# Last graph layer: the edge weights of a node group kept in the PSUM bank of its own sum

## The chip, the cores and the metric

The kernel runs on one core of a Trainium2 chip. The time is the device time of one execution in microseconds (us). Before the change the median of 13 runs is 5820.31 us (5806.52 to 5838.92).

The core has five engines that run their own instruction queues in order and wait for each other through semaphores: PE (matrix products, with PEld for the loading of its stationary operand), DVE (elementwise work and reductions), ACT (activations and copies), POOL (here mostly the issue of indirect DMAs, which gather rows of a table) and SP (plain DMAs). SBUF is the on-chip memory, PSUM the accumulator memory of PE: eight banks of 512 float32 values in each of 128 partitions.

## What is computed

The reference is a stack of four graph layers, each followed by a feed-forward layer, on 3125 nodes of 256 features. The change touches only the last graph layer, an attention over incoming edges with 8 heads of 32 features:

```python
h = (x @ W.T).reshape(n, H, D)                      # H = 8, D = 32
alpha = einsum(h_src, a_src) + einsum(h_dst, a_dst)
enc = relu(edge_attr @ edge_W.T + edge_b).reshape(-1, H, D)
alpha = alpha + sum(enc * h_dst, axis=-1)
alpha = where(alpha >= 0, alpha, 0.2 * alpha)
amax = segment_max(alpha, dst)
ex = exp(alpha - amax[dst])
denom = segment_sum(ex, dst)
attn = ex / maximum(denom[dst], 1e-10)
out = segment_sum(h_src * attn[..., None], dst).reshape(n, H * D) + bias
```

The result is added to x, normalised per node, and goes to the last feed-forward layer, which sends each node to two of eight experts.

## The kernel before

**Tiling.** The nodes are sorted by their number of incoming edges and cut into NT = 25 groups of 128, one node to a partition. Group g has KS[g] edge slots per node, from 41 in group 0 and 25 in group 1 down to 10 in group 24. A slot of a group is a 128 x 264 tile: 256 features of the edge's source and 8 partial scores. Slots go in chunks of C4 = 4, so there are 123 chunks: 104 of four slots, 6 of three, 6 of two and 7 of one.

**The loop.** `pipeline` (L1091) goes through all chunks of all groups in order, one chunk a turn. In a turn it first issues the gathers of up to two chunks: POOL fetches their slots from the table TA (L1082, 428 gathers of 128 rows in all), some six turns ahead and into 14 buffers `gt`. Then come the steps of the chunk and the score of the chunk before. The order in each engine's queue is the order in which the program is written out; no scheduler changes it.

- `enc_ahead` (L3101): ACT copies edge attributes (L3016), PE transposes them for eight slots into the first 128 columns of the PSUM tile `small` (L3026), ACT copies them out (L3035, L3039), and PE multiplies them with the edge weights (L3052) into `e_ps`, a PSUM tile with four buffers of one bank, two slots each.
- `score` (L3056): DVE takes relu and multiplies by the target's features, two slots an instruction (L3062), sums each head's 32 features into L, 8 scores a slot (L3065), and adds the gathered partial scores (L3066).
- When a group's last chunk has been scored, `tail` (L3075) is put beside the loop and advances by one step a turn. It adds the target's score and the leaky slope (L3077, L275) and calls `weigh`.

**`weigh`** (L1719) does the softmax and the weighted sum of one group. DVE adds a penalty for empty slots (L1725), takes the maximum (L1727, L1729) and subtracts it (L1730). ACT takes the exponential (L1734), for 8 heads in place, in the SBUF tile L. A turn later DVE sums the weights into `den` (L1739), and then in each turn multiplies one chunk of gathered features by its weights into an SBUF tile `wv` with four buffers (L1769). PE sums a chunk's four slots by four products with the identity into the PSUM tile `acc` (L1752; two records each in the trace, as the product is float32). In a turn the weighting of chunk k is written ahead of the matmuls of chunk k-1 (`summed`, L1748). Groups of more than six chunks, which are groups 0 and 1, take two chunks a turn. At the end `tail` divides by `den` (L3081 to L3084) and adds bias and sum to X (L3086, L3087). After each fifth group the normalisation of five groups runs beside the loop, with the product for the gate (L112) into further columns of `small`.

The helper `weigh` serves three layers. In the first layer (4 heads, then 1) it is given `exps`, and for 4 heads the exponentials are written to a PSUM tile `expo` of a bank of its own (L1734, read at L1739 and L1769). The last layer gives it none.

**PSUM in the last layer.** `tps2` one bank, `small` one, `e_ps` four, `acc` two buffers of 256 columns. A tile that is written by one engine and read by another is guarded by semaphores; `acc` has two buffers, so group g+2 reuses group g's.

Of the kernel before, what the change touches and what calls it, by code (L numbers as in the profile page):

```python
# [11 lines left out]
F32 = mybir.dt.float32  # L12
# [8 lines left out]
P = 128  # L21
D = 256
KD = D // P
N = 3125
NT = (N + P - 1) // P
# [16 lines left out]
def parts(tc, a, k, X, XNT):  # L42
# [17 lines left out]
    def spread(ap, shape):  # L60
        return ap[:, :, None].to_broadcast(shape)
# [318 lines left out]

    def first_of(pool, s, best, iota_e, E, name):

        oh = pool.tile([P, s.shape[1], E], F32, name=name)
        at = pool.tile([P, s.shape[1]], F32, name=name + "_at")
        nc.vector.tensor_tensor(oh, s, spread(best, [P, s.shape[1], E]), ALU.not_equal)
        nc.vector.scalar_tensor_tensor(oh, oh, 1000.0, iota_e, op0=ALU.mult, op1=ALU.add)
        nc.vector.tensor_reduce(at, oh, AX.X, ALU.min)
        nc.vector.tensor_tensor(oh, iota_e, spread(at, [P, s.shape[1], E]), ALU.is_equal)
        return oh

    def places(pool, E):
        iota_e = pool.tile([P, NT, E], F32, name="iota_e")
        nc.gpsimd.iota(iota_e, pattern=[[0, NT], [1, E]], base=0, channel_multiplier=0,
                       allow_small_or_imprecise_dtypes=True)
        return iota_e
# [629 lines left out]
E = 53125  # L1025
# [470 lines left out]
def quick(ctx: ExitStack, tc: tile.TileContext, a: dict, out: bass.AP, k):  # L1496
# [92 lines left out]
    E3, F3, R3 = 8, 1024, 2 * P  # L1589
# [123 lines left out]
    def chunks(g):  # L1713
        return [(c, min(C4, KS[g] - c)) for c in range(0, KS[g], C4)]
# [4 lines left out]
    def weigh(pool, psum, g, L, H, tiles, own=0, exps=None, bias=None):  # L1719


        K = KS[g]
        Z = K - own
        by_head = L.rearrange("p k h -> p h k")
        nc.vector.tensor_add(L[:, :Z, :], L[:, :Z, :], pen[:, OFF[g] : OFF[g] + Z, None].to_broadcast([P, Z, H]))  # L1725
        mx = pool.tile([P, H], F32, name="mx")
        nc.vector.tensor_reduce(mx, by_head, AX.X, ALU.max)  # L1727
        if not own:
            nc.vector.tensor_scalar_max(mx, mx, -0.5 * BIG)  # L1729
        nc.vector.tensor_sub(L, L, mx[:, None, :].to_broadcast([P, K, H]))  # L1730
        E = L
        if H == 4:
            E = exps(g, K * H).rearrange("p (k h) -> p k h", h=H)
        nc.scalar.activation(E, L, AF.Exp)  # L1734
        yield 0
        if own:
            nc.vector.tensor_scalar(E[:, Z, :], E[:, Z, :], 2.0, None, op0=ALU.mult)
        den = pool.tile([P, H], F32, name="den")
        nc.vector.tensor_reduce(den, E.rearrange("p k h -> p h k"), AX.X, ALU.add)  # L1739
        if H == 4:  # L1740
            nc.vector.reciprocal(den, den)
            nc.vector.tensor_mul(E, E, den[:, None, :].to_broadcast([P, K, H]))
        acc = psum.tile([P, D], F32, name="acc", bufs=2)
        if bias is not None:
            nc.tensor.matmul(acc, ident, bias, start=True, stop=False)
        held = []

        def summed():  # L1748
            for c, n, wv, t in held:
                for s in range(n):  # L1750
                    w, v = (wv[:, s, :P], t[:, s, :D]) if H == 1 else (ident, wv[:, s, :])
                    nc.tensor.matmul(acc, w, v, start=(c + s == 0 and bias is None), stop=(c + s == K - 1))  # L1752
            held.clear()


        todo = list(zip(chunks(g), tiles))
        per = 2 if len(todo) > 6 else 1
        for i in range(0, len(todo), per):
            made = []
            for (c, n), t in todo[i : i + per]:  # L1760
                wv = pool.tile([P, C4, D], F32, name="wv", bufs=4)
                if H == 1:
                    nc.vector.tensor_mul(wv[:, :n, :P], exps[:, None, :].to_broadcast([P, n, P]),  # L1763
                                         E[:, c : c + n, :].to_broadcast([P, n, P]))
                else:
                    x = t[:, :n, :D].rearrange("p s (h c) -> p s h c", h=H)
                    if H == 4:
                        x = t[:, :n, : D + H].rearrange("p s (h c) -> p s h c", h=H)[:, :, :, : D // H]
                    nc.vector.tensor_mul(wv[:, :n, :].rearrange("p s (h c) -> p s h c", h=H), x,  # L1769
                                         E[:, c : c + n, :, None].to_broadcast([P, n, H, D // H]))  # L1770
                made.append((c, n, wv, t))
            free = len(held) if H == 1 else len(made)
            summed()
            held.extend(made)
            yield free
        free = len(held) if H == 1 else 0
        summed()
        weighed[g] = acc, den
        yield free
# [3 lines left out]
    def gat(H, table, own_rows, att, fixed, expo, gp, mp, sp, psum, opened, finish, beside=None, ranked=0,  # L1783
# [55 lines left out]
        def tail(g):  # L1839
            if H == 1:  # L1840
                yield 0
            yield from weigh(sp, psum, g, st[g].L, H, list(st[g].tiles.values()), 1, exps, bias)
            st.pop(g)
            yield from finish(g, *weighed.pop(g))
# [384 lines left out]
    with tc.tile_pool(name="rt", bufs=1) as rt_pool:  # L2229
# [6 lines left out]
        H, C, INNER = 8, 64, 512  # L2236
# [183 lines left out]
        H, C = 4, 4  # L2420
# [6 lines left out]
        with tc.tile_pool(name="rg", bufs=12) as gp, tc.tile_pool(name="rs", bufs=2) as sp, \  # L2427
# [13 lines left out]
            def tail(g, acc):  # L2441
                nc.vector.scalar_tensor_tensor(X[:, g, :], acc, 0.5 ** 0.5, X[:, g, :], op0=ALU.mult, op1=ALU.add)
                nc.vector.tensor_add(X[:, g, :], X[:, g, :], hb)
                if g % BATCH < BATCH - 1:
                    return
                yield 0
                gs = range(g - BATCH + 1, g + 1)
                yield from norm_pieces(sp, psum, gs)
                tbs = []
                for g_ in gs:  # L2450
                    ps = psum.tile([P, HC], F32, name="hg_ps", bufs=2)
                    f.node_matmul(ps, g_, wg, slice(0, HC))
                    tb = sp.tile([P, GW], F32, name="tb", bufs=2 * BATCH)
                    tv = tb[:, : H * (C + 1)].rearrange("p (h c) -> p h c", h=H)
                    nc.vector.memset(tb, 1.0)
                    nc.vector.tensor_copy(tb.bitcast(I32)[:, H * (C + 3) : H * (C + 3) + 1], place[:, g_ : g_ + 1])
                    nc.scalar.copy(tv[:, :, :C], ps.rearrange("p (h c) -> p h c", h=H))
                    m = sp.tile([P, 2, HC], F32, name="m2")
                    nc.vector.tensor_mul(m, ps[:, None, :].to_broadcast([P, 2, HC]), at_r)
                    nc.vector.tensor_reduce(tb[:, H * (C + 1) : H * (C + 3)],  # L2460
                                            m.rearrange("p s (h c) -> p (s h) c", h=H), AX.X, ALU.add)
                    tbs.append(tb)
                    yield 0
                yield 0
                yield 0
                for g_, tb in zip(gs, tbs):
                    scatter(tc, "gm", gm, pid(g_), tb)
                    yield 0
# [453 lines left out]
    H, C = 8, 32  # L2922
# [17 lines left out]
    with tc.tile_pool(name="ag", bufs=abufs) as gp, tc.tile_pool(name="am", bufs=2) as mp, \  # L2940
# [39 lines left out]
        HS = lgs[:, :, :H]  # L2980

        tps2 = psum.tile([P, 2, KD, P], F32, name="tps2")
        small = psum.tile([P, P + NT * E3], F32, name="small")
        halves = itertools.cycle(range(2))
        turns = SimpleNamespace(tile=lambda *_, **__: tps2[:, next(halves), :, :])
        for gs in batches():
# [16 lines left out]
        tiles, Ls, atts, es, logits = {}, {}, {}, {}, {}  # L3003
# [71 lines left out]
        def tail(g):  # L3075
            L = Ls.pop(g)
            nc.vector.tensor_add(L, L, HD[:, g : g + 1, D:].to_broadcast([P, KS[g], H]))  # L3077
            f.leaky(L, L)
            yield from weigh(sp, psum, g, L, H, tiles.pop(g))
            acc, den = weighed.pop(g)  # L3080
            nc.vector.tensor_scalar_max(den, den, 1e-10)  # L3081
            nc.vector.reciprocal(den, den)
            h = sp.tile([P, D], F32, name="h")
            nc.vector.tensor_mul(h.rearrange("p (h c) -> p h c", h=H), acc.rearrange("p (h c) -> p h c", h=H),  # L3084
                                 den[:, :, None].to_broadcast([P, H, C]))
            nc.vector.tensor_add(X[:, g, :], X[:, g, :], bias)  # L3086
            nc.vector.tensor_add(X[:, g, :], X[:, g, :], h)  # L3087
            if g % BATCH == BATCH - 1:
                yield 0
                yield from norm_pieces(sp, turns, range(g - BATCH + 1, g + 1), XN, (gate, gated))  # L3090
                b = slice(g - BATCH + 1, g + 1)
                nc.sync.dma_start(top_xn[b.start * P : b.stop * P, :].rearrange("(t p) d -> p t d", p=P), XN[:, b, :])
# [195 lines left out]
```

## Time and profile before

| what | value |
|---|---|
| median of 13 runs | 5820.31 us |
| profiled execution: time, span | 5837.86 us, 5835.9 us |
| last layer: first gather, last accumulating matmul | 4603 us, 5325 us |
| busy over the span: PE, DVE, ACT, POOL | 58%, 53%, 21%, 49% |
| gathers of the last layer (L1082) | 428, 432.9 us, mean 1011 ns |
| weighting of the last layer (L1769) | 123, 138.8 us, mean 1135 ns |
| accumulation of the last layer (L1752) | 906 records, 289.7 us, mean 474 ns |
| scores (L3062) and their sums (L3065) | 233, 147.2 us; 123, 139.7 us |
| exponentials (L1734) in the last layer | 25, 8.1 us |
| sums of the weights (L1739) in the last layer | 25, 10.1 us |

How to read it: the span is one execution as the hardware profiler saw it, from its first to its last instruction. Busy times count the engines' own instructions, not waits. Groups are told by line, engine and operation, with a tile's name for its output and inputs; a line can be that of a helper, so L1769 stands in the page both for the first layer and for the last, and only a stretch of time tells them apart. "Idle before" is the time that the engine stood still just ahead of a group's instructions, with what ended it. The clock is the share of full speed that TensorE was granted.

### The profile page before, as it was taken

The numbers are of one execution on the slowest core, as the hardware profiler recorded it, in microseconds if no ns is written. First come the engines' busy times: TensorE is split into PE (matmuls) and PEld (weight loads), VectorE is DVE, ScalarE is ACT, GpSimd is POOL, SyncE is SP. The second block draws the span as 40 slices with busy tenths as digits, with TensorE's granted clock in tenths as the row PEclk, the third lists the DMA queues.
The fourth block names the chain that finished last, engine by engine and source line by source line (L and its number), as shares of the span: only waits on it lengthen the run. The fifth ranks groups of instructions, "written<-read, shape, count | busy, mean of one in ns | idle before, by whom it ended". The sixth has DMA issues, their size and how long they took to land.

```text
span 5835.9 us, 43920 instructions
## 1 busy us (share of the span) xinstructions
PE 3360.3 (58%) x12989; PEld 2304.6 (39%) x13034; DVE 3093.9 (53%) x6063; ACT 1219.2 (21%) x3088; POOL 2881.7 (49%) x3076
## 2 busy tenths in 40 slices
PE   2334553355487964545347556059679355556996
PEld 1223333234354532434124333035354233334885
DVE  4577877798675754651114331473441567876001
ACT  1222223455531200000013232121112101111221
POOL 4567664577765036675644535430403566661323
PEclk9676777676798976666668777579885677777998
DMA  4534342233321233332212221253324333332554
GB/s 122 158 103 108 107 114 83 79 98 110 100 31 43 113 95 93 87 87 76 29 35 77 51 60 25 67 155 103 119 79 122 98 88 87 92 90 69 190 191 161
DMA packets 320900, 553.70 MB, mean 95 GB/s; under 512 B 101962, under 2 KB 221885, under 8 KB 317311
## 3 DMA queue, kind: packets, MB, share of 16 engines
q0 software_dynamic: 124240, 295.98, 19.9%
q1 hardware_dynamic: 189973, 248.17, 12.9%
q10 hardware_dynamic: 6422, 6.48, 0.4%
q8 instruction: 112, 1.84, 0.1%
q14 instruction: 153, 1.25, 0.1%
HBM read 434.55 MB, written 118.86 MB: 95 GB/s over the span
## 4 chain that ended last, share of the span: by engine, by line
PE 25%; DVE 22%; issue 19%; another core or an unknown queue 14%; POOL 10%; DMA 3%; ACT 3%; SPq 0%; DVEq 0%; ACTq 0%; POOLq 0%
POOL gt L1082 5%; PE acc L2761 3%; PE hx_ps L112 3%; DVE m L1820 3%; DVE m L1828 3%; DVE wv L1769 3%; POOL rp_g L1082 3%; PE x_o L2626 3%; PE x_ps L2612 3%; PE acc L2764 2%; PE acc L1752 2%; PE acc L1863 2%; DVE m L3062 2%; DVE L L3065 1%
## 5 line engine op out<-in xcount | busy, mean ns | idle before, releaser
L1082 POOL DMA_INDIRECT gt<-T,recs x856 | 899.5, 1051 | 464.7 <-issue 335.8
L1752 PE MATMUL acc<-wv,ident 128*128 128x256 f32 x1812 | 562.2, 466 | 290.6 <-DVE wv L1769 217.3
L1082 POOL DMA_INDIRECT gt<-rel,relz x428 | 413.6, 966 | 436.8 <-issue 368.2
L1082 POOL DMA_INDIRECT gt<-gm,recs x428 | 405.5, 948 | 420.5 <-DVE L L275 207.1
L1752 PEld LDWEIGHTS acc<-wv,ident 128*128 128x128 f32 x1812 | 416.5, 237 | 411.9 <-DVE wv L1769 167.5
L1082 POOL DMA_INDIRECT gt<-TA,recs x428 | 432.9, 1011 | 277.7 <-issue 116.6
L1752 PE MATMUL acc<-gt,wv 128*128 128x256 f32 x906 | 301.0, 493 | 315.5 <-DVE wv L1763 213.5
L1863 PE MATMUL acc<-gt,ident 128*128 128x256 f32 x856 | 288.5, 472 | 173.3 <-issue 149.6
L2633 DVE TENSOR_TENSOR x_y<-x_o,x_b 128x512 f32<-128x512 f32 (+1 forms) x52 | 34.4, 670 | 638.4 <-remote 250.1
L1752 PEld LDWEIGHTS acc<-gt,wv 128*128 128x128 f32 x906 | 215.1, 248 | 394.3 <-issue 163.0
L2761 PE MATMUL acc<-XNT,adj_g 128*128 128x512 bf16 x955 | 331.3, 392 | 49.4 <-issue 40.0
L2612 PE MATMUL x_ps<-XNT,x_w 128*128 128x512 f32 (+1 forms) x448 | 243.3, 675 | 186.5 <-ACT x_h L2614 125.6
L1823 ACT ACTIVATE m<-m 128x1024 f32<-128x1024 f32 (+3 forms) x246 | 243.5, 990 | 507.6 <-DVE m L1820 271.0
L1820 DVE TENSOR_TENSOR m<-gt,R 128x1040 f32<-128x1040 f32 (+6 forms) x246 | 281.9, 1146 | 105.0 <-DMA gt<-T,recs 70.9
L2764 PE MATMUL acc<-F,adj_g 128*128 128x256 bf16 x1000 | 279.3, 280 | 38.1 <-issue 30.1
L1863 PEld LDWEIGHTS acc<-gt,ident 128*128 128x128 f32 x856 | 196.1, 237 | 253.4 <-issue 191.8
L1828 DVE TENSOR_TENSOR m<-m,fixed 128x1040 f32<-128x1040 f32 (+6 forms) x246 | 280.4, 1140 | 23.7 <-ACT m L1823 19.1
L1082 POOL DMA_INDIRECT gt<-gcn,z_i x120 | 119.4, 995 | 315.5 <-DVE F L2736 166.7
L2626 PE MATMUL x_o<-x_w,x_h 128*128 128x256 f32 x800 | 209.9, 405 | 70.0 <-issue 70.0
L2612 PEld LDWEIGHTS x_ps<-XNT,x_w 128*128 128x128 f32 x448 | 92.0, 230 | 279.5 <-issue 143.5
L3183 PE MATMUL fh_ps<-xt,w 128*128 128x256 f32 x896 | 201.0, 383 | 0.8 <-DVE xt L3175 0.8
L3196 PE MATMUL fo_ps<-w,ht 128*128 128x256 f32 x896 | 198.0, 379 | 0.0
(653 smaller groups left out, 7037.4 us busy)
## 6 DMA issues: line engine op xcount, KB each, us to landing
w<-in_L_ffn_W_dram SPq DMA_DIRECT2D x56, 1024.0 KB
adj_g<-adj SPq DMA_DIRECT2D x40, 800.0 KB
rel<-hx SPq DMA_DIRECT2D x25, 1024.0 KB
adj<-em_a SPq DMA_DIRECT2D x20, 800.0 KB
gt<-T,recs POOLq DMA_INDIRECT x856
y<-each_d SPq DMA_DIRECT2D x25, 512.0 KB
each_d<-x_y SPq DMA_DIRECT2D x24, 512.0 KB
R<-rr SPq DMA_DIRECT2D x25, 388.5 KB
```

The lines of the kernel that those rows point to most:

```text
L1082: return nc.gpsimd.indirect_dma_start(out=out_, out_offset=None, in_=table, in_offset=index(idx))
L1752: nc.tensor.matmul(acc, w, v, start=(c + s == 0 and bias is None), stop=(c + s == K - 1))
L1820: nc.vector.tensor_add(m[:, :n, :], st[g].tiles[c][:, :n, :W], st[g].R[1][:, None, :].to_broadcast([P, n, W]))
L1823: nc.scalar.activation(v, v, AF.Abs)
L1828: nc.vector.tensor_mul(m[:, :n, :], m[:, :n, :], att_row[:, None, :].to_broadcast([P, n, W]))
L1863: nc.tensor.matmul(accs[g], ident, t[:, s, :], start=False, stop=(last and s == n - 1))
L2612: nc.tensor.matmul(ps[:, :n], ws[e][0][:, c, f_ * P : (f_ + 1) * P], XNT[:, c, c0 : c0 + n], start=(c == 0), stop=(c == KD - 1))
L2626: nc.tensor.matmul(ps[:, j, :], ht[:, f_, (i + j) * P : (i + j + 1) * P], ws[e][1][:, f_, :], start=(f_ == 0), stop=(f_ == FC - 1))
L2761: nc.tensor.matmul(acc.rearrange("p s d -> p (s d)"), A[:, b, :], F12[:, b, :, :].rearrange("p s d -> p (s d)"), start=(b == 0), stop=Fals ...
L2764: nc.tensor.matmul(acc[:, 0, :], A[:, b, :], F3_[:, b, :], start=False, stop=(b == NT - 1), skip_group_check=True)
L3183: nc.tensor.matmul(ps[:, i, :], ld[j][1][:, c, (f_ + i) * P : (f_ + i + 1) * P], xt[j][:, c, :], start=(c == 0), stop=(c == KD - 1))
L3196: nc.tensor.matmul(ps[:, i, :], h[:, f_, i * P : (i + 1) * P], w2[:, f_, :], start=(f_ == 0), stop=(f_ == FC3 - 1))
```

## The change

The tile `acc` of the last layer becomes a whole bank of 512 columns, and is taken before the exponentials instead of after. Columns 0 to 255 are the sum as before; columns 256 onward take the group's weights, 8 to a slot, which ACT now writes there instead of to L. `den` and the weightings read them from there. Group 0 has 41 x 8 = 328 weights, more than the 256 free columns. Its weights go to the last 328 columns of `small`, which grows from 328 to 512 columns; the first 184 stay free of them. The first layer's code is as before.

```diff
         nc.vector.tensor_sub(L, L, mx[:, None, :].to_broadcast([P, K, H]))
+        acc = psum.tile([P, 512], F32, name="acc", bufs=2) if H == 8 else None
         E = L
         if H == 4:
             E = exps(g, K * H).rearrange("p (k h) -> p k h", h=H)
+        if H == 8:
+            room = acc[:, D : D + K * H] if K * H <= 512 - D else exps[:, 512 - K * H :]
+            E = room.rearrange("p (k h) -> p k h", h=H)
         nc.scalar.activation(E, L, AF.Exp)
...
-        acc = psum.tile([P, D], F32, name="acc", bufs=2)
+        acc = acc[:, :D] if H == 8 else psum.tile([P, D], F32, name="acc", bufs=2)
...
-        small = psum.tile([P, P + NT * E3], F32, name="small")
+        small = psum.tile([P, 512], F32, name="small")
...
-            yield from weigh(sp, psum, g, L, H, tiles.pop(g))
+            yield from weigh(sp, psum, g, L, H, tiles.pop(g), exps=small)
```

## Prediction

> **What bounds the kernel now.** I read first the page's chain of waits, then the busy times by stretch, the waits and the groups of the last graph layer alone, and last its timeline. One line of the chain:
>
> ```profile
> PE 25%; DVE 22%; issue 19%; another core or an unknown queue 14%; POOL 10%; DMA 3%; ACT 3%; SPq 0%; DVEq 0%; ACTq 0%; POOLq 0%
> ```
>
> No engine holds the kernel as a whole, so the stage that the change touches has to be read by itself. The last layer's edge work runs from 4603 us (first gather) to 5325 us (last accumulating matmul). Two of its stretches (columns: stretch, length, busy time and count of PE, PEld, DVE, ACT, POOL, then clock, DMA share, GB/s):
>
> ```profile
> 4900.00:5100.00 200.00, 123.29 (x448) 85.73 (x447) 162.15 (x304) 22.51 (x77) 132.00 (x128) 0.77 0.33 93
> 5255.00:5326.00 71.00, 49.02 (x181) 34.96 (x179) 64.09 (x147) 10.75 (x30) 10.66 (x16) 0.76 0.10 27
> ```
>
> DVE is busy 81% and 90%, PE 62% and 69%, POOL 66% and 15%. Who waits for whom, from 4660 us on (total, times, longest):
>
> ```profile
> DVE m L3062 <- remote: 55.8, 9, 16.6
> DVE wv L1769 <- remote: 23.1, 2, 14.5
> DVE L L3066 <- DMA gt<-TA,recs: 1.2, 1, 1.2
> ...
> POOL gt L1082 <- DVE wv L1769: 107.3, 25, 12.8
> ```
>
> POOL waits 107 us for DVE to give back gather buffers; DVE waits 1.2 us for gathers. So DVE sets the pace, apart from about 90 us in which it waits for something that the profile can't name ("remote", before instructions whose inputs are ready).
>
> **What is changed, part by part.** Set side by side, the two built programs have the same instructions in the same order on all five engines. What differs is where 25 exponentials (L1734) write, where 25 sums (L1739) and 123 weightings (L1769) read, and the semaphore waits that follow from it.
>
> *The weighting itself.* Its second operand moves from SBUF to PSUM. The first layer has this very form, its weights being in a PSUM tile:
>
> ```profile
> L1769 DVE TENSOR_TENSOR wv<-gt,expo 128x1024 f32<-128x1024 f32 x104 | 125.5, 1214 | 33.1 <-remote 24.0 <-issue 6.7
> L1769 DVE TENSOR_TENSOR wv<-gt,L 128x1024 f32<-128x1024 f32 x104 | 126.2, 1219 | 36.4 <-remote 23.1 <-PE e_ps L3052 13.3
> ```
>
> 1214 against 1219 ns: 104 x 5 ns is half a microsecond, taken as nothing. [...] Sums and exponentials: the same two layers have, at 88 elements, 250 ns from PSUM and 301 ns from SBUF (L1739; four and eight outputs), and 248 and 277 ns (L1734, a write to PSUM and to SBUF). 25 x 30 ns is under 1 us, hidden in ACT's idle time; without cover it would be a gain of 0.7 us.
>
> *The gathers.* One turn of the pipeline in the timeline (start, length, engine, line, operation):
>
> ```profile
> 4943.10 1.22 DVE L1769 TENSOR_TENSOR wv<-gt,L 128x1024 f32<-128x1024 f32 x1
> 4943.27 1.87 POOL L1082 DMA_INDIRECT gt<-TA,recs  x1 [0.30 <-issue]
> 4944.24 1.02 DVE L3062 SCALAR_TENSOR_TENSOR m<-e_ps,XN 128x512 f32<-128x512 f32 x2
> ...
> 4944.37 1.99 PE L1752 MATMUL acc<-wv,ident 128*128 128x256 f32 x8 [1.39 <-DVE wv L1769]
> 4945.29 0.95 DVE L3065 TENSOR_REDUCE L<-m 128x24 f32<-128x768 f32 x1
> 4945.45 0.95 POOL L1082 DMA_INDIRECT gt<-TA,recs  x1 [0.30 <-issue]
> ...
> 4946.43 1.22 DVE L1769 TENSOR_TENSOR wv<-gt,L 128x1024 f32<-128x1024 f32 x1
> 4946.70 1.77 POOL L1082 DMA_INDIRECT gt<-TA,recs  x1 [0.30 <-issue]
> ...
> 4947.70 1.99 PE L1752 MATMUL acc<-wv,ident 128*128 128x256 f32 x8 [0.79 <-DVE wv L1769]
> ```
>
> A gather is 0.95 us; one that starts while a weighting runs is 1.77 or 1.87. Counted over the stage, 66 of 428 start during a weighting, 44 of them are slow, and their excess over 0.95 sums to 25.4 us. In the first layer, whose weighting reads PSUM, 91 gathers start during one and none is slow. So the change takes 25 us off POOL. But POOL is the engine that waits: DVE gets at most its 1.2 us, and a little where the chain crosses to POOL for a few gathers (4982 to 4987, 5066 to 5083, 5202 to 5219). Bounds 0 and 8 us, taken 2, near the waits' row.
>
> *The new waits.* The built program treats the bank as one thing. The weights now share it with the sum, so (a) the four matmuls of chunk k-1 (L1752), which waited for weighting k-1, wait for weighting k, the last reader before them in the order; and (b) weighting k+1 on DVE waits until those matmuls are done. Before, four wv buffers kept (b) off. Behind the waiting weighting stand DVE's next scores (L3062, L3065), and for them POOL's buffers; behind the waiting matmuls stand the attribute transposes (L3026) and encodings (L3052).
>
> [...] The sum uses only the waits as built.
>
> Price of (b): from weighting k to k+1 DVE needs 1.22 (the weighting) + 0.06 (end to matmul, 4940.50 to 4940.56) + 1.99 (the batch) + up to 0.10 (back) = 3.37 us. What DVE has there now, from the start times: 3.81 where a full chunk of four is scored between, 3.33 with three, 2.72 with two, 2.19 with one (4943.10 to 4946.43; 4782.94 to 4785.66; 4846.44 to 4848.63). So full turns hide it, and the short ones lose 0.04, 0.65 and 1.18. Of the 57 such intervals in groups 2 to 22, most contain other work or gaps; three at 2.72 and four near 2.2 are bare: 2.0 + 4.7 = 6.7 us. That is with warm matmuls. After an idle spell the same eight records take 3.6 to 3.8 us (4878.73: 3.78), and then even a full turn loses 1.3. Putting the length of the batch recorded behind each weighting in place of 1.99 gives 19.6 us in 18 intervals. Bounds 6.7 and 19.6; I take 14, since the weighting's wait keeps PE no idler than now, but PE is cold after each DVE gap.
>
> *Groups 0 and 1* go two chunks a step, so eight matmuls, 3.6 to 6.6 us, stand between pairs. From the starts 4704.47, 4708.30, 4713.29 and 4716.63 the last weighting of group 0 would slip 6.4 us, and group 1 some 3; group 0's weights also share the bank of the transposes. DVE has gaps of 14.5 and 8.6 us before and 13.3 us after. Bounds 0 and 10, taken 5.
>
> *The end* has no other work to hide it:
>
> ```profile
> 5318.31 1.22 DVE L1769 TENSOR_TENSOR wv<-gt,L 128x1024 f32<-128x1024 f32 x1
> ...
> 5319.67 1.97 PE L1752 MATMUL acc<-wv,ident 128*128 128x256 f32 x8 [0.96 <-DVE den L3081]
> ...
> 5321.08 1.82 DVE L1769 TENSOR_TENSOR wv<-gt,L 128x1024 f32<-128x1024 f32 x2
> 5322.36 2.86 PE L1752 MATMUL acc<-wv,ident 128*128 128x256 f32 x12 [0.72 <-DVE wv L1769]
> ```
>
> The last two groups run their last two weightings back to back. Now the batch stands between: in group 24 the batch of 5319.67 starts only at 5322.3, the third weighting at 5324.4, and the last 12 records end at 5327.9, not 5325.2: +2.7. Group 23 loses 2.3 the same way: 5 in all. The routing behind it waits for the last group, so all of it counts.
>
> **Sum:** 14 + 5 + 5 = 24. Less 4 (bounds 0 and 8) that DVE's unnamed gaps give back, where a late instruction finds its block already there; less 2 for gathers: +18. On the profiled execution's 5837.9 us (span 5835.9) that is 5856; it stands 17.6 above the median 5820.3, to which the same +18 gives **5838 us**, 0.3% slower.
>
> **Rivals.**
> *Swallowed.* DVE's unnamed gaps (55.8 + 23.1 + 11.7 + 2.9 = 93.5 us) come at fixed moments, and every stall before one disappears. Only the end stays: 5825. For: the gaps are seven times the stalls. Against: they fall at about ten places, and the stalls at others.
> *PE becomes the pace.* 27 batches of eight records are now over 3.0 us long. If each costs the full 1.3, not only the bare ones: 35 + 6.7 + 5 + 5 - 4 - 2 = +46, so 5866. For: DVE now feels each hiccup of PE. Against: batches in long intervals have room.
> *Faster.* The gathers set the pace after all and the whole 25.4 us comes back, with only the end's 5 lost: 5800. It decides from the point where DVE would otherwise wait at L3066 for landings. For: POOL runs without a break over long stretches. Against: 1.2 us of such waits.
>
> **Chances.** Forecast 0.52, swallowed 0.22, PE 0.13, faster 0.13. About 0.2% (11.6 us) is what a measurement here tells from no change: slower is above 5832. A little of the forecast's case (0.04) lies below that: slower 0.61, same 0.26, faster 0.13. The forecast's own range is 5820.3 + 6.7 + 0 + 5 - 8 - 8 = 5816 to 5820.3 + 19.6 + 10 + 5 = 5855; it already takes in swallowed, and to leave out no more than 2 in 10 I stretch it to 5814 and 5861.
>
> **What would show it.** In the profile after: weightings of 1.21 to 1.22 us; no slow gather starting in one, POOL's mean for gt<-TA near 0.95; a new wait DVE wv <- PE acc of 15 to 30 us in total; PE waiting for weighting k, not k-1; POOL's wait for wv still about 100 us or more; the stage longer by about 18 us, the last matmul some 5 us further from the last den. The forecast is wrong if DVE's wait for acc is under 8 us, if POOL's wait for wv shrinks along with the stage, or if the weighting's duration moves.

## The result and the profile after

Changed: 5887.51 us (median of 14 runs, 5866.58 to 5902.29). Before, beside it: 5826.84 us (62 runs, 5806.52 to 5852.16). The ratio is 1.0103 with a 95% interval of 1.0091 to 1.0115: slower by some 60 us, where +18 was forecast and 5861 was the upper end of the range. The profiled execution's span went from 5835.9 to 5892.9 us, +57.0.

Where these 57 us lie, by the starts of the same weightings in both traces: the first weighting of the last layer comes 5.2 us later (work that is the same in both), from there to the last accumulating matmul 658.2 us have become 711.1 (+52.9), and what follows is 1.1 us shorter. Within the stage: groups 0 and 1 +16.4, groups 2 to 22 +26.8, groups 23 and 24 +9.7.

The busy times of the stage, before and after (columns: stretch, length, busy time and count of PE, PEld, DVE, ACT, POOL, then clock, DMA share, GB/s):

```profile
4660.00:5325.00 665.00, 381.62 (x1342) 260.21 (x1342) 510.65 (x962) 70.70 (x236) 391.66 (x390) 0.75 0.30 83
```

```profile
4665.00:5383.00 718.00, 381.33 (x1342) 259.23 (x1342) 510.57 (x962) 72.27 (x237) 365.84 (x391) 0.74 0.28 76
```

DVE works the same 510.6 us in both, so all 53 us are idle time of DVE. POOL works 25.8 us less, and nobody gains by it. The groups of the stage and the waits after (second fence: total, times, longest):

```profile
L1773 DVE TENSOR_TENSOR wv<-gt,acc 128x1024 f32<-128x1024 f32 x94 | 114.0, 1216 | 46.3 <-PE acc L1756 24.6 <-remote 15.7 <-issue 6.0
L1773 DVE TENSOR_TENSOR wv<-gt,small 128x1024 f32<-128x1024 f32 x10 | 11.8, 1215 | 23.1 <-remote 23.1
```

```profile
DVE wv L1773 <- remote: 58.4, 8, 14.6
DVE m L3066 <- remote: 56.3, 18, 10.8
DVE wv L1773 <- PE acc L1756: 32.3, 23, 3.8
...
PE acc L1756 <- DVE wv L1773: 208.3, 57, 15.7
...
POOL gt L1082 <- DVE wv L1773: 156.2, 41, 13.7
```

The same wait of the sums before:

```profile
PE acc L1752 <- DVE wv L1769: 59.2, 32, 7.7
```

The weighting itself is as long as before (1216 and 1215 against 1219 ns). The wait that was forecast is there: DVE's weightings wait 32.3 us for the sums, the sums 208.3 us for weightings (59.2 before). What was not forecast is that the unnamed waits grew too: DVE's were 55.8 + 23.1 + 11.7 + 2.9 = 93.5 us and are 58.4 + 56.3 + 12.1 + 3.5 + 3.3 = 133.6. Before, the weighting waited twice for something unnamed, now eight times. The waits named as PE's encodings fell from 28.9 to 0.7 us. So most of the waiting of the scores for PE is still there, and a new one of the weightings has come on top.

Two steady turns after (start, length, engine, line, operation):

```profile
5030.23 1.22 DVE L1773 TENSOR_TENSOR wv<-gt,acc 128x1024 f32<-128x1024 f32 x1 [1.19 <-PE acc L1756]
5031.50 1.99 PE L1756 MATMUL acc<-wv,ident 128*128 128x256 f32 x8 [0.56 <-DVE wv L1773]
5033.53 1.22 DVE L1773 TENSOR_TENSOR wv<-gt,acc 128x1024 f32<-128x1024 f32 x1 [0.50 <-issue]
...
5034.81 1.99 PE L1756 MATMUL acc<-wv,ident 128*128 128x256 f32 x8 [0.88 <-issue]
```

Weighting, sums and weighting follow each other hand to hand, 3.30 us apart. And the end:

```profile
5374.67 1.21 DVE L1773 TENSOR_TENSOR wv<-gt,acc 128x1024 f32<-128x1024 f32 x1
...
5376.03 3.60 PE L1756 MATMUL acc<-wv,ident 128*128 128x256 f32 x8 [2.53 <-DVE wv L1773]
5379.66 0.69 DVE L1773 TENSOR_TENSOR wv<-gt,acc 128x512 f32<-128x512 f32 x1 [3.78 <-PE acc L1756]
...
5380.41 2.86 PE L1756 MATMUL acc<-wv,ident 128*128 128x256 f32 x12 [0.78 <-DVE wv L1773]
```

The last weighting waits 3.78 us for a batch that takes 3.60, not the 1.97 of before. PE had just stood idle for 2.53 us. The clock (the figure before the last two) of the first steady batch and of this one:

```profile
5031.50:5033.49 1.99, 1.99 (x9) 1.63 (x10) 1.41 (x3) 0.00 (x0) 1.47 (x2) 1.00 0.33 87
5376.03:5379.63 3.60, 3.60 (x8) 2.49 (x8) 0.00 (x0) 0.00 (x0) 0.00 (x0) 0.54 0.00 0
```

A batch of eight records is called cold here when it runs at about half the clock and takes over 3 us. In this trace such batches follow idle time: 27 of the 29 batches of four slots that come behind an idle PE of 2.4 us or more are cold, and 4 of the 60 that come behind less than 1 us. Before it was 5 of 9 and 22 of 72, so the idle time just ahead of a batch is not all that decides.

### The profile page after: what moved, and what is told of

Read it like the earlier page. It is cut to its first block, busy times and chain, and to the rows that moved or that the text cites. A ratio compares the mean times of both kernels' runs of the same rounds, so it can differ in the third digit from the quotient of the medians.

```text
span 5892.9 us, 43923 instructions
## 1 busy us (share of the span) xinstructions
PE 3369.8 (57%) x12989; PEld 2309.4 (39%) x13034; DVE 3094.3 (53%) x6063; ACT 1219.0 (21%) x3088; POOL 2856.1 (48%) x3076
## 4 chain that ended last, share of the span: by engine, by line
PE 26%; DVE 24%; issue 19%; another core or an unknown queue 13%; POOL 9%; DMA 3%; ACT 3%; DVEq 0%; POOLq 0%; SPq 0%; ACTq 0%
POOL gt L1082 5%; PE acc L2765 3%; DVE m L1824 3%; PE acc L1756 3%; DVE wv L1773 3%; DVE m L1832 3%; PE hx_ps L112 3%; PE x_ps L2616 3%; POOL rp_g L1082 3%; PE x_o L2630 3%; PE acc L2768 2%; DVE m L3066 2%; DVE L L3069 1%; DVE L L1837 1%
## 5 line engine op out<-in xcount | busy, mean ns | idle before, releaser
L1756 PE MATMUL acc<-wv,ident 128*128 128x256 f32 x1812 | 579.1, 478 | 446.0 <-DVE wv L1773 358.4
L1082 POOL DMA_INDIRECT gt<-TA,recs x428 | 406.9, 951 | 344.8 <-DVE wv L1773 156.2
```

What stands on the lines that cost most here:

```text
L1082: return nc.gpsimd.indirect_dma_start(out=out_, out_offset=None, in_=table, in_offset=index(idx))
```

## The experiments

The rounds of runs fell on five chips, and these are of two kinds. On three the kernel before takes 5799 to 5829 us, as it does in the first comparison; on two it takes 5127 and 5129. So only ratios to the kernel before on the same chip are compared.

**First theory: the loop of two waits** (sums of chunk k-1 held until weighting k has read, weighting k+1 held until they are done). Four kernels, on a chip where the kernel before takes 5127.15 us. Sums emitted first:

```diff
         for i in range(0, len(todo), per):
+            if H == 8:
+                summed()
             made = []
```

> The changed kernel, with the matmuls of chunk k-1 emitted ahead of the weighting of chunk k instead of behind it. Every engine has the same instructions in the same order; the bank is still shared, and weighting k still waits for the matmuls of chunk k-1, but these no longer wait for weighting k. Theory L (the loop: matmuls held until the next weighting has read, and the weighting after it until they are done, costs the 60 us): most of it goes, 5827 + 5 at the last two groups + 0 to 10 = 5832 to 5842, ratio 1.001 to 1.003. Rival W (any wait of a weighting for matmuls in the bank costs it): 5870 or more, ratio 1.008 and up. Rival O (the operand in PSUM, through faster gathers or slower neighbours, costs it, and no wait): 5887, ratio 1.010.

Measured: 5188.02 us, ratio 1.0120 [1.0105, 1.0136]. The first theory (1.001 to 1.003) falls: without the one half of the loop the loss in per cent is as large as in the first comparison (the changed kernel itself was not run on this chip). The program as built shows why: weighting k now waits for the sums of chunk k-1, and these for weighting k-1. As this program and the changed one are built, sums and weightings in the shared bank wait for each other, so either of the two orders leaves one handover in each turn: here PE's sums wait 77.8 us in 55 waits for weightings, and DVE's weightings 80.1 us in 37 for sums. In DVE's waits of this stage nothing is unnamed on this chip:

```profile
DVE wv L1775 <- PE acc L1756: 80.1, 37, 5.9
```

The timeline of this kernel shows one of them:

```profile
4261.86 0.16 DVE L3079 TENSOR_TENSOR lg<-small,bg 128x8 f32<-128x8 f32 x1
4262.07 1.02 PE L112 MATMUL small<-wg,XNT 128*128 128x8 f32 x4 [3.69 <-DVE lg L3079]
...
4262.95 0.67 PE L1573 MATMUL tps<-ident,XN 128*128 128x128 f32 x2
...
4263.41 3.62 PE L1756 MATMUL acc<-wv,ident 128*128 128x256 f32 x8
...
4267.07 1.22 DVE L1775 TENSOR_TENSOR wv<-gt,acc 128x1024 f32<-128x1024 f32 x1 [5.05 <-PE acc L1756]
```

The sums stand in PE's queue behind the gate and a transpose; the gate waits 3.69 us for DVE; then the batch takes 3.62 us, at a granted clock of 0.50; and DVE waits 5.05 us for it. The direct path of weighting and sums is only a part of this round. Worked out from the starts in this trace: had each of the 37 batches begun 0.06 us behind its weighting, up to 57 of the 80.1 us would be gone; had each taken 1.99 us, up to 29 (20 of them are cold); the two overlap.

Weights in a bank of their own, made room for by putting both accumulators in one bank (the companion has this alone):

```diff
+        if H == 8 and g:
+            E = wts[:, g % 2, : K * H].rearrange("p (k h) -> p k h", h=H)
...
-        acc = psum.tile([P, D], F32, name="acc", bufs=2)
+        acc = exps[:, g % 2, :] if H == 8 else psum.tile([P, D], F32, name="acc", bufs=2)
...
+        acc2 = psum.tile([P, 2, D], F32, name="acc2")
+        wts = psum.tile([P, 2, D], F32, name="wts")
```

> Weights of groups 1 to 24 in a PSUM bank of their own (two halves by group), room for it made by putting both accumulators in one bank; group 0's weights in SBUF. Weightings read PSUM as in the changed kernel, but share no bank with matmuls. Theory L and rival W: no loss by the operand, so the time of the kernel with both accumulators in one bank (its companion here) within 6 us, ratio to before 0.998 to 1.003. Rival O: about 40 to 60 us above that companion, ratio 1.008 or more. If the gathers set the pace after all: 10 to 25 us below the companion.

> The kernel before with both accumulators in one PSUM bank and nothing else: the price of making room. A group's first matmul now waits until the group before has been read (once per group, 24 times). All theories: 0 to 10 us, ratio 1.000 to 1.002.

Measured: own bank 5111.69 us, 0.9966 [0.9952, 0.9979]; companion 5126.67 us, 0.9997 [0.9988, 1.0006]. The room is free, and the operand in PSUM is no loss here but a gain of 15 us, as was expected for the case that the gathers set the pace (10 to 25 below the companion). Rival O falls. In the companion DVE waits 15.8 us in 20 waits for landings of gathers, with the own bank 2.7 in 4.

Two buffers for weighted rows, weights in SBUF:

```diff
-                wv = pool.tile([P, C4, D], F32, name="wv", bufs=4)
+                wv = pool.tile([P, C4, D], F32, name="wv", bufs=2 if H == 8 else 4)
```

> The kernel before, weights in SBUF, with two buffers for weighted rows instead of four: weighting k+1 waits for the matmuls of chunk k-1, as in the changed kernel, but these do not wait for weighting k. Theory L: 0 to 10 us, ratio 1.000 to 1.002. Rival W: this wait alone gives most of the loss, 40 us or more, ratio 1.007 and up. Rival O: 0 to 10 us.

Measured: 5134.74 us, 1.0015 [1.0006, 1.0024]. Weighting k+1 waits for the same sums as in the changed kernel, but these may start one turn earlier. Rival W (1.007 and up) falls: not any wait for the sums is dear. With a turn of slack the wait costs 8 us; without it, in the kernel with the sums first, the loss is 61 (there with the operand in PSUM).

**Second theory: one handover a turn, and it is the wait, not the bank.** Four kernels on another chip (before 5798.79 us). The changed kernel again; with group 0's weights in SBUF; with only groups 2 to 22 sharing:

```diff
-        if H == 8:
+        if H == 8 and 2 <= g < NT - 2:
```

and the waits alone, in SBUF, with one buffer for weighted rows per parity of the group:

```diff
+            if H == 8:
+                summed()
...
+                wv = pool.tile([P, C4, D], F32, name=f"wv{g % 2}", bufs=1) if H == 8 and per == 1 else \
+                    pool.tile([P, C4, D], F32, name="wv", bufs=2 if H == 8 else 4)
```

> The changed kernel as it is, beside the others of this round. Theory R (one handover a turn: with the bank shared, the matmuls and the weightings of a group can only take turns, and the matmuls stand behind encodings and transposes that wait for ScalarE, so the whole round trip between DVE and PE falls into every turn): the same as with the sums emitted first, since either order has one handover a turn, so ratio 1.010 to 1.014. If the first theory (the loop of two waits) still has something to it: clearly above the 1.012 of that kernel, 1.016 or more.

> The changed kernel with group 0's weights left in SBUF, so that the bank of the transposes holds no weights. Theory R: group 0 has two chunks a turn and is one of 25, so 0 to 10 us below the changed kernel. Rival T (the waits on the transposes' bank, which hold PE for 25 us in the profile of the changed kernel, are the main price): 30 us or more below it.

> The changed kernel with the weights of groups 0, 1, 23 and 24 left in SBUF, so that only the steady middle (groups 2 to 22) shares its banks. Theory R: 5 to 20 us below the changed kernel, ratio to before still 1.007 or more. Rival E (the price lies at the two ends of the stage, where nothing covers a wait): ratio 1.003 or less.

> The kernel before, its weights in SBUF, with the sums emitted ahead of the weighting and a single buffer for weighted rows per group of each parity (two where a turn takes two chunks): weighting k waits for the matmuls of chunk k-1 in every turn, exactly the waits of the shared bank with the sums first, but DVE and PE never use a PSUM bank together. Theory R: the waits are the whole price, so ratio 1.009 to 1.015. Rival H (the chip itself holds up one engine while the other uses the bank): clearly less, 1.004 or below.

Measured: changed 5853.18 us, 1.0087 [1.0068, 1.0106]; group 0 out of it 5840.96, 1.0075 [1.0058, 1.0093]; steady middle only 5830.32, 1.0057 [1.0042, 1.0072]; waits alone 5844.50, 1.0075 [1.0058, 1.0092]. By the medians the +54 divides into 12 for group 0 (a little over what was expected, and its interval overlaps), 11 for groups 1, 23 and 24, and 32 for the middle. The ratios of the changed kernel, of the middle and of the waits alone lie 0.0013 to 0.0015 below their expected bounds, inside their intervals; the middle alone is 23 us below the changed kernel, where 5 to 20 were expected. The rival that the ends hold the price falls, though 23 of the 54 us do lie in groups 0, 1, 23 and 24. That a hold-up in the bank itself is the price falls too: with the weights in SBUF, the waits of the order with the sums first lose 46 us. That order is not the changed kernel's; but in the changed kernel's trace the weightings (1216 ns) and the sums at full clock (1.99 us) are no longer than before, either.

**Is it PE's queue?** The sums moved to the head of PE's turn, in front of transposes, encodings and gate (before 5829.48 us on this chip):

```diff
         def enc_ahead(g, c, n, last):
+            for s in early:
+                s()
```

> The changed kernel with the matmuls of chunk k-1 moved to the head of PE's turn, in front of the transposes, the encodings and the gate instead of behind them; bank, weights and handovers stay. Theory Q (the price comes from what PE has queued between a weighting and its sums: with the sums first in the queue the round trip lies beside the scoring on DVE): ratio to before 0.998 to 1.003. Rival D (weighting and batch alone, with cold batches of 3.4 to 3.8 us, are too long for a turn, wherever the sums stand): 1.006 or more, within 0.004 of the 1.009 to 1.010 of the changed kernel.

> The kernel before with the same move of the sums to the head of PE's turn, weights in SBUF: what the move does by itself. Theory Q and rival D: little, since four buffers for weighted rows keep the sums off DVE's path, ratio 0.997 to 1.003. If the encodings, which now come later in the turn, are DVE's real supply: above 1.004.

> The kernel with the weights in a PSUM bank of their own, once more, beside the others of this round and perhaps on another chip. If its gain came from gathers that no longer run slow: 0.995 to 0.999 again. If that gain needs a chip on which DVE waits for nothing but gathers: 0.998 to 1.003 here.

> Weights in a bank of their own and the sums at the head of PE's turn. No wait between weighting and sums is left for the move to shorten: within 0.003 of the kernel with the own bank. If the move helps through PE's order alone, as much below it as the kernel before with the move is below the kernel before.

Measured: changed with the move 5871.65 us, 1.0082 [1.0061, 1.0104]; before with it 5845.10, 1.0031 [1.0015, 1.0048]; own bank 5845.29, 1.0032 [1.0018, 1.0046]; own bank with the move 5868.08, 1.0082 [1.0062, 1.0102]. Two expectations failed: theory Q's of 0.998 to 1.003 for the changed kernel with the move, and that the move makes no odds to the own bank (it adds 0.005). The kernel before with the move and the own bank lie just above their bounds of 1.003. So the move costs 16 to 23 us by itself, and the own bank is slower than before on this chip. The changed kernel's 1.0082 is thus what the direct-path rival forecast, but not for its reason: the kernel without any sharing has the same 1.0082. The move also puts the sums ahead of the next weighting, so it has to be compared with the kernels that have the sums first. With the sums at the head of PE's queue, sharing the bank adds 3.6 us to the own bank, nothing that can be told apart; with the sums first but behind the rest of the queue it added 76 on the quicker chip (5111.69 to 5188.02), and the waits alone add 48 on a chip like this one (next part). That speaks for the queue in the kernels with the sums first. The comparison goes across chips, it doesn't reach the changed kernel's own order, and the move loses by itself what it saves in waits.

**How the loss divides.** Room, operand, sharing, and the waits alone, on one more chip (before 5822.44 us); the edits are those above:

> Both accumulators in one bank, weights in SBUF, on the same chip as the next three. Theory R: nothing, 0.998 to 1.002, so that what the own bank costs is the operand's. Rival A (on a chip on which PE crawls, the wait of a group's first matmul for the group before costs): 1.002 to 1.005, and the own bank's price is this one.

> Weights in a bank of their own. On a chip where DVE has waits without a name: 1.001 to 1.005 as on the last one, on a chip without: 0.995 to 0.998. Theory R: in either case clearly below the changed kernel, by 0.5% or more.

> The changed kernel. Theory R: what it has over the own bank is the handover, 0.5 to 0.8% on a chip with unnamed waits, 1.2 to 1.6% on one without (there the sums emitted first were 1.5% over the own bank).

> The waits alone, weights in SBUF. Theory R: 1.006 to 1.009 on a chip with unnamed waits, 1.010 to 1.015 on one without. Rival H (a hold-up in the shared bank itself): 1.004 or less.

| kernel | us | ratio to before | 95% interval | adds |
|---|---|---|---|---|
| accumulators in one bank | 5823.97 | 1.0007 | 0.9992 to 1.0023 | room: +2 |
| weights in a bank of their own | 5845.07 | 1.0046 | 1.0024 to 1.0067 | operand in PSUM: +21 |
| changed | 5897.66 | 1.0118 | 1.0092 to 1.0144 | sharing: +53 |
| waits alone, weights in SBUF | 5870.66 | 1.0081 | 1.0060 to 1.0101 | +48 on before |

The room costs nothing that can be told from noise, so rival A falls. Sharing is the larger part, and the copy of the waits in SBUF, in the order with the sums first, is worth about the same. The 53 us are 0.9% of the own bank's time, where 0.5 to 0.8% were expected, and they include group 0, whose weights the own bank leaves in SBUF (12 us in the round before). The smaller part is the operand, and its sign depends on the chip: +21 here, -15 on the chip of the first round.

**Why the operand helps or hurts.** One small memset on POOL after each chunk's gathers, with the weights in their own bank, gives POOL back the time that the faster gathers save:

```diff
+            nc.gpsimd.memset(idle, 0.0)
```

> Weights in a bank of their own, and after each chunk's gathers a small memset on POOL (123 of about 0.2 us, some 25 us in all, about what the slow gathers took before). If the earlier gathers make the difference: back to the kernel before, 0.998 to 1.002, on either kind of chip. If something else in the operand does: the same as its companion without memsets within 0.002.

> The companion, weights in a bank of their own, no memsets: 1.002 to 1.006 on a chip with unnamed waits, 0.995 to 0.998 on one without.

Measured, on the second of the two quicker chips (before 5129.14 us): padded 5120.85 us, 0.9985 [0.9976, 0.9994]; companion 5110.51 us, 0.9965 [0.9951, 0.9979]. The memsets take 223 ns each, and DVE's waits for landings go from 2.7 back to 9.7 us. So 10 of the 19 us hang on POOL's time for the gathers. The ratio lies at the lower edge of the first expectation (0.998) and at the upper edge of the second (0.002 above the companion), so it doesn't decide between them, and the other 8 us have no shown cause. Why the operand costs 21 us on the slow kind of chip stays open: this pair did not fall on one. In the traces there, DVE's waits in the stage grow from 137 us (both accumulators in one bank) to 154 (weights in their own), nearly all of it in what the profile calls "issue" (3.3 to 16.9 us): time in which it names nothing that was waited for.

## Why the prediction was wrong

- *What bounds the stage.* Right: DVE's busy time is 510.6 us before and after, and everything lost is idle time of DVE.
- *The weighting.* Right: 1215 and 1216 ns from PSUM.
- *The gathers.* What was forecast of them came: some 60 gathers start during a weighting and none is slow, the mean fell from 1011 to 951 ns, and POOL's wait for weightings grew (107.3 to 156.2 us) instead of shrinking. Before, with both operands of the weighting in SBUF, 36 of the gathers that start during one take over 1.2 us, the longest 1.99, and none of the 354 others over 1.14; after, with one operand in PSUM, the longest beside a weighting takes 0.95. What in the operand makes the difference was not shown. But the price, "bounds 0 and 8 us, taken 2" as a gain, had the wrong sign: with no sharing, the operand costs 21 us on one such chip (5823.97 to 5845.07), and operand and room 16 on another. The range had no loss in it. (Counted by the starts in the trace, 74 gathers rather than 66 began during a weighting before; their excess over 0.95 us is 25.5 us, as forecast.)
- *The new waits, the step that failed.* The forecast said: "from weighting k to k+1 DVE needs 1.22 (the weighting) + 0.06 (end to matmul) + 1.99 (the batch) + up to 0.10 (back) = 3.37 us", and took 14 us between 6.7 and 19.6 for the middle, "since the weighting's wait keeps PE no idler than now". In groups 2 to 22 weightings wait 22.3 us for sums by name (24.0 and 23.7 in the two other profiled executions of the changed kernel), more than the upper bound. The 3.37 is right where the batch runs at full clock (3.30 at 5030.23 to 5033.53). But the wait does keep PE idler, just ahead of its sums: these now wait 208.3 us for weightings (59.2 before). Cold batches are only a few more, but now DVE waits for them to their end. Of the 23 named waits in the whole stage 17, with 22.0 of the 32.3 us, are for batches at a clock of 0.50 to 0.55; the four for batches at full clock cost about 1 us each. Worked out from the starts: had each batch taken 1.99 us, up to 20.4 of the 32.3 us would be gone; had each begun 0.06 us behind its weighting, 3.7. So in the changed kernel what stands ahead of the sums in PE's queue is a small part of these waits, unlike in the kernel with the sums first. All this is read from traces; no run changed the clock. Sharing as a whole cost 53 us on one chip, where 14 + 5 + 5 had been summed.
- *The unnamed waits.* "Less 4 that DVE's unnamed gaps give back" was wrong: nothing came back. The gaps are waits for PE: by the trace's semaphore events all 14 before and 30 of the 31 after end within 0.1 us of an update of the semaphore that PE's instructions raise, often some us after the last PE instruction on record has ended. In groups 2 to 22 they grew by as much (70.3 to 81.0 us) as DVE's named waits for PE other than those for sums shrank (16.5 to 5.8), so of the +26.8 there, 22.3 are the named waits for sums and 4.3 "issue". The rest of the 40 us by which they grew lies in groups 0 and 1. They differ from trace to trace: 134, 101 and 140 us in the three traces of the changed kernel, 121 and 82 in two with the weights in their own bank. Why PE's answers come late there stays open.
- *Groups 0 and 1.* Direction right, size not: 5 taken, 16.4 by the trace. The waits for sums, which the forecast priced, are 3.5 us of it; DVE's other waits for PE, named and unnamed, rose from 38.4 to some 49. That group 0's weights share the bank of the transposes was named but not priced by itself: PE's transposes once wait 25.4 us for a weighting there, and without group 0 in PSUM the kernel was 12 us faster on another chip.
- *The end.* 5 taken, 9.7 by the trace, 6.5 of it named waits for sums. The last matmul is 13.4 us behind the last den, 7.1 before: +6.3 where 5 was said. The mechanism was right, but the batch that decides was cold (3.60 us at a clock of 0.54).
- *Rivals.* "PE becomes the pace", 5866, was nearest, 21 us short; it saw the cold batches, which are 34 of 85 batches of eight records from group 2 on and were 27 of 81. It let each cost 1.3 us; the trace shows up to 20 us for the named waits. "Swallowed" and "faster" had nothing for them on this chip. On the other kind of chip the "faster" rival's reason is real, and worth 15 to 19 us once the bank isn't shared.

## What to carry to other kernels

Before two engines are made to share a bank or a buffer that lets them only take turns, walk the whole round from one engine's use to its next. Ask at what clock the answering instructions will run after the pause that the wait itself puts ahead of them (1.99 or 3.78 us for the same batch here), and what stands *ahead* of them in the other engine's queue; the bare durations at full clock were only a lower bound here (3.37 us forecast for the round, and 22.3 us of named waits in groups 2 to 22 where 6.7 to 19.6 had been worked out). One turn of slack hid most of such a round in these runs (8 us lost with it; 46 to 61 without, on different chips), and emitting the two in the other order didn't create it (5188.02 us, ratio 1.0120). The waits without a name, larger here than the effect forecast (93.5 us against 18), were no reserve: they were waits for the other engine.

## What the runs showed of the hardware

The chips differ by 700 us in the kernel before, and nearly all of it is waiting. In the first trace of the kernel before DVE has some 635 us of unnamed waits in all, in every trace from the two quicker chips 0. In the traces from the other chips PE at times starts instructions one by one, at multiples of 0.70 us, while waiting for nothing that the profile names (kernel before, group 0):

```profile
4679.90 0.38 PE L1752 MATMUL acc<-wv,ident 128*128 128x256 f32 x1 [1.34 <-issue]
4682.70 0.26 PE L3026 MATMUL small<-ident_b,attr 128*32 128x128 bf16 x1 [2.43 <-issue]
4684.80 0.59 PE L3052 MATMUL e_ps<-EW,att 128*128 128x512 bf16 x1 [1.84 <-issue]
4687.60 0.58 PE L3052 MATMUL e_ps<-EW,att 128*128 128x512 bf16 x1 [2.21 <-issue]
```

DVE's weighting then comes at 4694.62, after an unnamed wait of 14.51 us. Some 390 starts on PE, matmuls and weight loads taken together, lie 0.70 or 1.40 us apart (within 12 ns) in the first trace of the kernel before, 17 in the companion with both accumulators in one bank on a quicker chip. Of the twelve idle gaps of DVE over 3 us from 4660 us on, nine end only when POOL has stopped for want of a buffer and the last gather in flight has landed, 1.3 to 3.8 us after it; in the changed kernel it is twelve of twenty, 1.0 to 4.5 us after it. Whether one causes the other wasn't tried. What makes PE crawl no run here shows.
